# A three-layer graph network: fetching edge lists three nodes at a time, where one block's odd edges are summed, and which engine divides

## The chip, the cores and the metric

The kernel runs on one core of a Trainium2 chip. The core has five engines, each with an instruction queue of its own that it works off in order: TensorE (PE: matmuls, with weight loads shown as PEld), VectorE (DVE), ScalarE (ACT), GpSimd (POOL) and SyncE (SP). SP and ACT issue plain transfers, POOL issues gathers, which fetch one row of a table for each of 128 partitions. The time is in device microseconds for one execution. Before the change it is 3873.78 us, the median of nine runs (3866.43 to 3889.36).

## The reference

The inputs are 6250 nodes with 256 features, 100,000 edges (`src`, `dst`, random and sorted by `dst`), and the weights of three attention layers. Each layer sums, over the edges that end in a node, rows of their source nodes, weighted by a softmax over those edges:

```
xl, xr = x @ Wl, x @ Wr                      # 4 heads of 64 (GATv2, two layers)
e      = leaky_relu(xl[src] + xr[dst])
logits = sum over a head of e * att
alpha  = softmax of logits over the edges with the same dst
out    = sum over those edges of alpha * xl[src], + b
x      = layernorm(x + gatv2(elu(gatv2(x))))   # edges of a node to itself added
x      = layernorm(x + gat(x))                 # 8 heads of 32, softmax again
```

The kernel sums over a node's edges with unnormalised exponentials and divides once by their sum. So "the division" below is 256 numbers per node, multiplied by four reciprocals (one for each head), and not a division of each edge.

## The kernel before

**Blocks and columns.** Nodes are sorted by their number of edges, most first, and cut into 49 blocks of 128. A block lays its nodes on the 128 partitions. Block b has `cols[b]` columns, one edge of every node in each: 27 in block 0, and fewer in the later ones. A node's list can hold CM = 38 sources. Block 0 has some nodes with more than 27 edges; those surplus edges have no column (at most 128 in all, FEW = 11 a node) and are done on the side, one edge to a partition: `find_few` (L1240), `few_logits` and `few_sum` (L1293). Places in a list that no edge fills name an extra row (`far`) made so that its weight comes out as zero.

**The prologue, `make_plan` (L712).** The order of its instructions is written out by hand, and each engine follows it. It computes:
- the number of edges of each node (`count`, [128 x 49]). A node stands at partition `node & 127`, column `node >> 7`; `part` splits a node number in this way, and one-hot matmuls into `ph` add the counts up;
- where each node's edges begin in the sorted `src` (`begin_i`, L993), by a matmul over partitions and a running sum over the 49 columns;
- the lists: 49 gathers on POOL (L998), one for each column, each with 38 numbers for 128 nodes, from `list_d`, a copy of `src` in DRAM;
- each node's place in the order by degree: `key`, one-hots `oh`, running sums `cum`, then `place_f`. ACT's queue writes it as one number to a row of the table `xl1_d` (L1058);
- the reverse, which node stands at which place: one-hots `to_hi` (L1071), `given` (L1076), `to_lo` (L1080) and 49 matmuls into `pp` give `node_i`;
- `lacking` (L1006) marks the list places that no edge fills, `fill` (L1013, L1016) puts `far` there with a predicated copy and writes the lists to `near_d` through SP's queue, nine columns (1152 nodes) at a time, six times. A row of `near_d` is the list of one node (38 numbers) with its 256 features behind it, so that one gather fetches both;
- 49 `tables` (L834 to L846): a block of x is transposed and multiplied by Wl1, and written to `xl1_d`. They are placed in groups between the other work;
- checks that the lists and columns suffice (`wrong`, `bad`, summed over partitions by a matmul into `pb`; `many`, L1114; `fits`, L1116), and the weights of the other products (`right`, `left`).

**The layers, `tile_by_degree`.** POOL fetches a node's list row (`near_r`, L1607), and then column by column the rows of the sources (`g`, L1235): 128 rows of 1 KB to a gather, into tiles of up to nine columns, nine tiles in all. A tile is free for new gathers when all readers of its old content are through. For each block of the first two layers:
- DVE: maximum with `xr` (leaky relu in another form), times `att`, sum over each head (L1508 to L1510): the logits `lg`; then the largest logit of a node, `top` (L1374);
- ACT: exponentials of the four heads (L1381), which also give their sums `den`; DVE takes the reciprocal (L1585);
- DVE multiplies the rows by their weights in place (L1412); ACT does this for the last few columns of the block (L1411, four multiplications a column);
- PE adds the columns up, one matmul with the identity for each (L1419), into `acc`, for which there is one buffer.

The block before is finished inside the next one. ACT computes `h = acc * den` with four multiplications, one for each head (`scaled`, L1539), from PSUM; DVE adds the bias (L1546) or, in the second layer, x (L1660). In `layer2` this is called through `middle()`: after the logits, and ahead of `weights`, so on ACT's queue it stands ahead of the exponentials. In block 1 `middle()` also does `few_sum` for block 0 ahead of it: ACT copies the surplus edges' weights, a matmul brings them to one edge a partition (`few_w`, L1298), three DVE operations (L1303 to L1307) weight the rows, and a matmul (L1311) adds the result to `acc`. The third layer has the same structure, with 8 heads, and its sums and its division on DVE.

Of the kernel before, what the change touches and what calls it, by code (L numbers as in the profile page):

```python
# [714 lines left out]
def make_plan(  # L715
# [21 lines left out]

    one = ctx.enter_context(tc.tile_pool(name="plan_one", bufs=1))
# [7 lines left out]
    list_d = dram.tile([-(-E // CM) * CM + CM], I32, name="list_d")  # L746
# [124 lines left out]
    if rest:  # L871
# [9 lines left out]
    nothing = filled_tile("nothing", [1, list_d.shape[0] - E], 0, I32)  # L881
# [3 lines left out]
    nc.scalar.dma_start(list_d[E:].unsqueeze(0), nothing)  # L885
    nc.scalar.dma_start(
        list_d[:E].rearrange("(a b) -> a b", a=a), src.rearrange("(a b) -> a b", a=a)
# [4 lines left out]
    ranks = iota("ranks", [P, CM], [[1, CM]])  # L892
    ones = filled_tile("ones_f", [P, P], 1.0)
# [48 lines left out]
    for what in "lar":  # L942
# [4 lines left out]
    nc.vector.tensor_scalar(  # L947
        part[:, 0, :], run_i, SHIFT, P - 1, op0=OP.logical_shift_right, op1=OP.bitwise_and
    )
    nc.vector.tensor_single_scalar(part[:, 1, :], run_i, SHIFT + 7, op=OP.logical_shift_right)  # L950
# [27 lines left out]

    pc = ps.tile([P, 2, NB], F32, name="pc", tag="ph")
    nc.tensor.matmul(pc[:, 0, :], ones, count, start=True, stop=True)  # L980
    nc.tensor.matmul(pc[:, 1, :], above, count, start=True, stop=True)
# [3 lines left out]
    block = one.tile([P, NB], F32, name="block")  # L985
    nc.vector.tensor_copy(block, pc[:, 0, :])
    upto = one.tile([P, NB], F32, name="upto")
    nc.vector.tensor_tensor_scan(upto, ones_k[:, :NB], block, 0.0, op0=OP.mult, op1=OP.add)
    from_f = one.tile([P, NB], F32, name="from_f")
    nc.vector.tensor_sub(from_f, upto, block)  # L990
    nc.vector.tensor_add(from_f, from_f, pc[:, 1, :])
    begin_i = one.tile([P, NB], I32, name="begin_i")
    nc.vector.tensor_scalar(begin_i, from_f, float(E), 0.0, op0=OP.min, op1=OP.max)  # L993
    near = one.tile([P, NB, CM], I32, name="near")
    no = one.tile([P, NB, CM], I32, name="no")
    listed = list_d.rearrange("(a b) -> a b", b=CM)
    for k in range(NB):
        nc.gpsimd.indirect_dma_start(  # L998
            out=near[:, k, :], out_offset=None, in_=listed,
            in_offset=bass.IndirectOffsetOnAxis(ap=begin_i[:, k : k + 1], axis=1),  # L1000
        )
    spans = [(k, min(NB, k + 9)) for k in range(0, NB, 9)]

    def lacking(k0, k1):
        shape = [P, k1 - k0, CM]
        nc.vector.tensor_tensor(  # L1006
            no[:, k0:k1, :], ranks[:, None, :].to_broadcast(shape),
            count[:, k0:k1].unsqueeze(2).to_broadcast(shape), op=OP.is_ge,
        )

    def fill(k0, k1):
        shape = [P, k1 - k0, CM]
        nc.vector.copy_predicated(  # L1013
            near[:, k0:k1, :], no[:, k0:k1, :], far[:, None, :].to_broadcast(shape)
        )
        nc.sync.dma_start(  # L1016
            near_d[k0 * P : k1 * P, :CM].rearrange("(k p) c -> p k c", p=P).bitcast(I32),
            near[:, k0:k1, :],
        )


    tables(1)
# [3 lines left out]
    )  # L1026
    ohf = oh.rearrange("p k b -> p (k b)")
# [3 lines left out]
    for c0, c1 in cuts:  # L1031
        pk = ps.tile([P, 512], F32, name="pk", bufs=2)
        nc.tensor.matmul(pk[:, : c1 - c0], ones_b, ohf[:, c0:c1], start=True, stop=True)
        nc.vector.tensor_tensor_scan(
            cum[:, c0:c1], ones_k[:, : c1 - c0], pk[:, : c1 - c0],
            cum[:, c0 - 1 : c0] if c0 else 0.0, op0=OP.mult, op1=OP.add,
        )
    tables(2)
    for c0, c1 in cuts:
        pk = ps.tile([P, 512], F32, name="pk", bufs=2)  # L1040
        nc.tensor.matmul(pk[:, : c1 - c0], less, ohf[:, c0:c1], start=True, stop=True)
        nc.vector.tensor_add(cum[:, c0:c1], cum[:, c0:c1], pk[:, : c1 - c0])
    tables(12)
# [13 lines left out]
    with nc.allow_non_contiguous_dma(reason="one number to a row"):  # L1057
        nc.scalar.dma_start(  # L1058
            xl1_d[:NP, W2:].rearrange("(b p) w -> p b w", p=P), place_f.unsqueeze(2)
        )  # L1060
# [6 lines left out]
    nc.sync.dma_start(xl1_d[NP:], nobody[:, 0, : W2 + 1])  # L1067

# [15 lines left out]
    for b in range(NB):  # L1084
        nc.tensor.matmul(pp, to_lo[:, b, :], given[:, b], start=b == 0, stop=b == NB - 1)
    for k in spans:
        lacking(*k)
    fill(*spans[0])
    fill(*spans[1])
# [3 lines left out]
        node_i, got[:, 1, :], float(P), got[:, 0, :], op0=OP.mult, op1=OP.add  # L1093
# [4 lines left out]
    wrong = one.tile([P, KE + NB + 1], F32, name="wrong")  # L1098
    nc.vector.tensor_tensor(wrong[:, : KE - 1], dst_e[:, : KE - 1], dst_e[:, 1:], op=OP.is_gt)
    nc.vector.tensor_tensor(wrong[:, KE - 1 : KE], dst_e[:, KE - 1 :], next_e, op=OP.is_gt)  # L1100
    nc.vector.tensor_tensor(wrong[:, KE : KE + NB], got[:, 2, :], most, op=OP.is_gt)
    nc.vector.tensor_scalar(
        wrong[:, KE + NB :], upto[:, NB - 1 :], float(E), None, op0=OP.not_equal
# [6 lines left out]
    tables(4)  # L1110
    pb = ps.tile([P, 2], F32, name="pb", tag="ph")
    nc.tensor.matmul(pb, ones, bad, start=True, stop=True)
    many = one.tile([P, 1], F32, name="many")
# [3 lines left out]
    right(0)  # L1117
    left(1, nc.vector)
    right(1)
    fill(*spans[2])  # L1120
# [6 lines left out]
    fill(*spans[3])  # L1127
# [10 lines left out]
    for k in spans[4:]:  # L1138
        fill(*k)
# [3 lines left out]
def tile_by_degree(  # L1143
# [149 lines left out]
    def few_sum(work, ps, acc, wt, S, H, width, first):  # L1293
# [511 lines left out]
```

## Time and profile before

| what | value |
|---|---|
| median of 9 runs | 3873.78 us (3866.43 to 3889.36) |
| the profiled execution | 3868.99 us, its span 3867.1 us |
| mean granted TensorE clock | 0.67 |
| prologue: first list gather, last list gather's end, first instruction of the layers on POOL | 40.25, 114.1, 154.82 us |
| layer 1, blocks 0 to 48 | about 205 to 1530 us |
| layer 2 | about 1530 to 2730 us |
| layer 3 | to 3867 us |
| division on ACT (L1539) | 392 instructions, 92.4 us |
| exponentials (L1381) | 392 instructions, 117.5 us |
| DVE before the reciprocals (L1585) | 77.1 us idle over 98 blocks |
| transfers over the span | 395.63 MB, 102 GB/s |

The layers' times are those at which DVE computes `top` of their first block. In a row of the groups, the numbers after the count are the busy time in us, the mean time of one instruction in ns, and the time that the engine stood idle just before them with what ended most of it. In a row of the timeline they are the start, the duration (of all x-many together), engine, line and operation, and in brackets the idle time before with what ended it. "issue" means that nothing is seen that the engine waited for, "remote" that the releaser is not known.

### The profile page before, as it was taken

Reading aid. Unit: us, or ns where it says so; the run is one execution under the profiler, and the core shown is the slowest. Engines: PE = TensorE matmul, PEld = TensorE weight load, DVE = VectorE, ACT = ScalarE, POOL = GpSimd, SP = SyncE. Lnnn points to the kernel's source line nnn. Section 1 sums busy time; section 2 is a strip of 40 time slices with the busy share of each in tenths; the row PEclk is TensorE's granted clock in tenths of the full one; section 3 lists DMA queues with packets and bytes.
Section 4 is the critical chain, followed back from the end, with each engine's and each line's share of the span. In section 5 each row is a group of like instructions: output and inputs, shape, how many; then the busy total and the mean of one; then the engine's idle time right before and its main releaser. Section 6 shows DMA issues by size and latency. Waiting matters only on the chain.

```text
span 3867.1 us, 23945 instructions
## 1 busy us (share of the span) xinstructions
PE 1514.0 (39%) x5129; PEld 1123.4 (29%) x5130; DVE 2801.1 (72%) x2550; ACT 1187.1 (31%) x4568; POOL 2535.4 (66%) x2613
## 2 busy tenths in 40 slices
PE   5325565556676663455644556554000000000000
PEld 4214444434554542344433444443000000000000
DVE  6248897758888876798877889985776565656665
ACT  2114444434455542344434444553000000000000
POOL 6466666666666654666666666653777777777774
PEclk8657788778888886677766767776555555555555
DMA  8433333333343333334434444432333333333332
GB/s 189 103 92 101 101 102 99 105 98 102 103 106 102 103 88 95 104 105 109 107 105 109 111 112 109 118 102 69 104 108 101 97 96 96 98 97 96 97 96 58
DMA packets 196126, 395.63 MB, mean 102 GB/s; under 512 B 63036, under 2 KB 115514, under 8 KB 195956
## 3 DMA queue, kind: packets, MB, share of 16 engines
q0 software_dynamic: 122048, 338.04, 33.3%
q1 hardware_dynamic: 66226, 54.22, 4.8%
q10 hardware_dynamic: 7698, 1.74, 0.4%
q8 instruction: 45, 0.74, 0.1%
q14 instruction: 109, 0.89, 0.1%
HBM read 353.82 MB, written 40.42 MB: 102 GB/s over the span
## 4 chain that ended last, share of the span: by engine, by line
issue 26%; POOL 19%; PE 18%; DVE 16%; ACT 10%; another core or an unknown queue 9%; DMA 2%; DVEq 0%; SPq 0%; ACTq 0%; POOLq 0%
POOL g L1235 18%; PE acc L1419 13%; DVE z L1508 4%; DVE z L1509 4%; ACT g L1411 3%; PE pm L1362 3%; DVE lg L1510 3%; ACT wt L1381 2%; DVE g L1412 2%; POOL out L1745 1%; ACT h L1539 1%; DMA g<-xl_d,near_r 1%; DVE weighted L1432 1%; PE pt L1355 1%
## 5 line engine op out<-in xcount | busy, mean ns | idle before, releaser
L1235 POOL DMA_INDIRECT g<-xl_d,near_r x1569 | 1491.1, 950 | 826.2 <-issue 441.9
L1419 PE MATMUL acc<-g,ident 128*128 128x256 f32 x3408 | 1068.1, 477 | 828.2 <-issue 313.2
L1419 PEld LDWEIGHTS acc<-g,ident 128*128 128x128 f32 x3408 | 794.6, 242 | 1095.3 <-issue 519.3
L1235 POOL DMA_INDIRECT g<-whs_d,near_r x766 | 794.2, 1037 | 286.7 <-issue 250.8
L1411 ACT ACTIVATE g<-g,by 128x64 f32<-128x64 f32 x2056 | 561.2, 338 | 459.9 <-issue 456.8
L1508 DVE TENSOR_TENSOR z<-g,pr 128x1820 f32<-128x1820 f32 (+4 forms) x234 | 497.2, 2125 | 31.8 <-remote 10.2
L1509 DVE TENSOR_TENSOR z<-z,at 128x1820 f32<-128x1820 f32 (+4 forms) x234 | 497.5, 2126 | 8.1
L1510 DVE TENSOR_REDUCE lg<-z 128x28 f32<-128x1820 f32 (+4 forms) x234 | 497.3, 2125 | 8.1
L1441 DVE TENSOR_REDUCE acc_v<-weighted 128x256 f32<-128x4096 f32 (+15 forms) x49 | 343.7, 7014 | 16.2 <-remote 8.3
L1412 DVE TENSOR_TENSOR g<-g,wt 128x1792 f32<-128x1792 f32 (+8 forms) x234 | 348.5, 1506 | 5.9 <-ACT sd L1455 2.2
L1391 ACT ACTIVATE wt<-lg 128x128 f32<-128x128 f32 (+17 forms) x49 | 14.0, 285 | 850.8 <-DVE top L1374 347.5
L1715 DVE TENSOR_TENSOR lg<-g,s_r 128x56 f32<-128x56 f32 (+4 forms) x111 | 22.4, 214 | 314.8 <-DMA g<-whs_d,near_r 295.3
L1432 DVE TENSOR_TENSOR weighted<-g,wt 128x1792 f32<-128x1792 f32 (+4 forms) x111 | 226.6, 2056 | 0.1
L1357 ACT COPY xT<-pt 128x256 f32<-128x256 f32 x147 | 54.9, 374 | 504.6 <-PE pt L1355 301.0
L1381 ACT ACTIVATE wt<-lg,top 128x19 f32<-128x19 f32 (+14 forms) x392 | 117.5, 300 | 155.2 <-issue 79.9
L1362 PE MATMUL pm<-wcat,xT 128*128 128x260 f32 x392 | 119.6, 456 | 34.4 <-ACT xT L1357 27.4
L1660 DVE TENSOR_TENSOR h<-h,near_r 128x256 f32<-128x256 f32 x49 | 20.8, 425 | 146.7 <-ACT h L1539 106.1
L1546 DVE TENSOR_TENSOR h<-h,fixed_r 128x256 f32<-128x256 f32 x49 | 20.9, 427 | 142.9 <-issue 62.0
L1362 PE MATMUL pm<-wh_cat,xT 128*128 128x272 f32 x196 | 84.1, 569 | 86.3 <-ACT xT L1357 45.8
L1362 PEld LDWEIGHTS pm<-wcat,xT 128*128 128x128 f32 x392 | 84.4, 227 | 63.0 <-ACT xT L1357 40.7
L1539 ACT ACTIVATE h<-acc,den 128x64 f32<-128x64 f32 x392 | 92.4, 332 | 22.8 <-PE acc L1311 22.8
L1362 PE MATMUL pl<-wcat,xT 128*128 128x260 f32 x196 | 60.9, 437 | 70.8 <-ACT xT L1357 49.2
(232 smaller groups left out, 1563.2 us busy)
## 6 DMA issues: line engine op xcount, KB each, us to landing
g<-xl_d,near_r POOLq DMA_INDIRECT x1569
g<-whs_d,near_r POOLq DMA_INDIRECT x766
whs_d<-row SPq DMA_DIRECT2D x49, 132.0 KB
xl_d<-xl SPq DMA_DIRECT2D x49, 130.0 KB
xl_d<-row SPq DMA_DIRECT2D x49, 130.0 KB
xr_d<-row SPq DMA_DIRECT2D x49, 130.0 KB
two<-xl_d SPq DMA_DIRECT2D x49, 130.0 KB
two<-xr_d SPq DMA_DIRECT2D x49, 130.0 KB
```

Of the source, the lines that this page charges most:

```text
L1235: nc.gpsimd.indirect_dma_start(out=g[:, j + own - s0, :width], out_offset=None, in_=table, in_offset=source(of, b, j),)
L1362: nc.tensor.matmul(pm, xT[:, c, :], w[:, c, :], start=c == 0, stop=c == 1)
L1381: nc.scalar.activation(wt[:, :, h], lg[:, :S, h], AF.Exp, bias=top[:, h : h + 1], accum_out=den[:, h : h + 1],)
L1411: nc.scalar.mul(g4[:, t, h, :], g4[:, t, h, :], by[:, t - m, h : h + 1])
L1412: nc.vector.tensor_mul(g4[:, :m], g4[:, :m], wt[:, s0 : s0 + m, :].unsqueeze(3).to_broadcast([P, m, H, F // H]),)
L1419: nc.tensor.matmul(acc, ident, g4[:, t], start=s0 + t == 0, stop=s0 + t == S - 1 and not more)
L1432: nc.vector.tensor_mul(prod[:, s0 - base : s1 - base, :].rearrange("p t (h d) -> p t h d", h=H), g[:, :n, :F].rearrange("p t (h d) -> p t ...
L1441: nc.vector.reduce_sum(part, prod[:, : s1 - base, :].rearrange("p s f -> p f s"), axis=AX.X)
L1508: nc.vector.tensor_max(z, g[:, :n, :W2], xr[:, None, :].to_broadcast([P, n, W2]))
L1509: nc.vector.tensor_mul(z, z, at[:, None, :].to_broadcast([P, n, W2]))
L1510: nc.vector.reduce_sum(lg[:, s0:s1, :], z.rearrange("p t (h d) -> p t h d", h=H2), axis=AX.X)
L1539: nc.scalar.mul(per_head(h, H2)[:, k, :], per_head(acc, H2)[:, k, :], den[:, k : k + 1])
```

## The change

*The lists.* A node now stands at partition `node // 49`, column `node % 49`; the quotient is had by a multiplication and a shift (`by`, `down`). So the 49 nodes of a partition are consecutive, and their edges lie one after another in `list_d`. Where a partition's edges begin is a matmul over the row sums (`total`), where a node's begin within the partition a running sum (`within`). POOL fetches 17 pieces for each partition, each for three nodes (SEGS, STEP) and of 133 numbers (LONG). A node's list starts somewhere in the piece: at the mean of 16 edges a node before it, and an offset of −32 to 31 from that. DVE moves each list to its place: `off_i` is the offset in 6 bits; copies with the mean's shift, and for each bit from 32 down to 1 a predicated copy that shifts those lists by that power of two whose bit is set (`moved`). 32 zeros stand ahead of the edges in `list_d` for this. A check is added that no offset is out of range. `fill` writes to `near_d` from POOL's queue instead of SP's, nine consecutive nodes to a partition, and all six fills stand together after the shifts. The tables are spread anew: 12 of them behind the write of `place_f` instead of ahead of it, and all that remain ahead of the check's matmul `pb`. The loads for the third layer's weights and the biases come behind all tables.

*The columnless edges.* `few_sum` runs in block 0, behind its weights, and its closing matmul into `acc` behind the block's sums. In the third layer the same function is called, and the matmul follows it as before.

*The division.* `end` multiplies `acc` by `den` with one DVE instruction for all four heads, behind `weights` of the next block; `middle` and `scaled` are gone.

```diff
-    list_d = dram.tile([-(-E // CM) * CM + CM], I32, name="list_d")
+    list_d = dram.tile([-(-(LEAD + E) // LONG) * LONG + LONG], I32, name="list_d")
...
-    nc.vector.tensor_scalar(
-        part[:, 0, :], run_i, SHIFT, P - 1, op0=OP.logical_shift_right, op1=OP.bitwise_and
+    nc.vector.tensor_single_scalar(part[:, 1, :], run_i, SHIFT, op=OP.logical_shift_right)
+    nc.vector.tensor_single_scalar(part[:, 0, :], part[:, 1, :], float(by), op=OP.mult)
+    nc.vector.tensor_single_scalar(part[:, 0, :], part[:, 0, :], down, op=OP.logical_shift_right)
+    nc.vector.scalar_tensor_tensor(
+        part[:, 1, :], part[:, 0, :], -float(NB), part[:, 1, :], op0=OP.mult, op1=OP.add
     )
-    nc.vector.tensor_single_scalar(part[:, 1, :], run_i, SHIFT + 7, op=OP.logical_shift_right)
...
-    for k in range(NB):
-        nc.gpsimd.indirect_dma_start(
-            out=near[:, k, :], out_offset=None, in_=listed,
+    piece_of = one.tile([P, SEGS, LONG], I32, name="piece_of")
+    listed = list_d.rearrange("(a b) -> a b", b=LONG)
+    for k in range(SEGS):
+        nc.gpsimd.indirect_dma_start(
+            out=piece_of[:, k, :], out_offset=None, in_=listed,
             in_offset=bass.IndirectOffsetOnAxis(ap=begin_i[:, k : k + 1], axis=1),
...
+    for k in range(STEP):
+        for first_at in (0, LEAD):
+            data = piece_of[:, :, MEAN * k + first_at : MEAN * k + first_at + WIDE]
+            if first_at == 0:
+                nc.vector.tensor_copy(moved[:, :, k, :], data)
+            else:
+                nc.vector.copy_predicated(
+                    moved[:, :, k, :],
+                    bit[:, BITS - 1, :, k : k + 1].to_broadcast([P, SEGS, WIDE]), data,
+                )
...
+    for k in range(BITS - 2, -1, -1):
+        n = CM + (1 << k) - 1
+        nc.vector.copy_predicated(
+            every[:, :, :n], bits[:, k, :].unsqueeze(2).to_broadcast([P, SEGS * STEP, n]),
+            every[:, :, 1 << k : (1 << k) + n],
+        )
...
-        nc.sync.dma_start(
-            near_d[k0 * P : k1 * P, :CM].rearrange("(k p) c -> p k c", p=P).bitcast(I32),
+        nc.gpsimd.dma_start(
+            near_d.rearrange("(p k) c -> p k c", k=NB)[:, k0:k1, :CM].bitcast(I32),
             near[:, k0:k1, :],
...
     for k in spans:
         lacking(*k)
-    fill(*spans[0])
-    fill(*spans[1])
+        fill(*k)
+    tables(4)
...
-    tables(4)
+    tables(NB)
     pb = ps.tile([P, 2], F32, name="pb", tag="ph")
...
-                middle()
...
-            def scaled(acc, den):
+            def end(b, acc, den):
                 h = work.tile([P, F], F32, name="h")
-                for k in range(H2):
-                    nc.scalar.mul(
-                        per_head(h, H2)[:, k, :], per_head(acc, H2)[:, k, :], den[:, k : k + 1]
-                    )
-                return h
+                nc.vector.tensor_mul(
+                    per_head(h, H2), per_head(acc, H2),
+                    den.unsqueeze(2).to_broadcast([P, H2, D2]),
+                )
...
-                rows, cut, wt, new = attend(b, middle)
+                rows, cut, wt, new = attend(b)
                 if b:
-                    rest = end(b - 1, h[0])
+                    rest = end(b - 1, acc, den)
                 else:
-                    few_wt = wt[0]
+                    few = few_sum(work, pst, wt[0], cols[0] + 1, H2, D2 + 1)
...
                 acc = weighted_sum(
                     ps1, rows, cut, wt, H2, D2 + 1, between, b == 0,
                 )
+                if b == 0:
+                    nc.tensor.matmul(acc, edges_of, few, start=False, stop=True)
```

## The prediction

> **What bounds the kernel now.** I read the totals and the groups by line first, then three stretches of the timeline: the prologue, block 1 of the first layer, and an ordinary block.
>
> ```profile
> PE 1514.0 (39%) x5129; PEld 1123.4 (29%) x5130; DVE 2801.1 (72%) x2550; ACT 1187.1 (31%) x4568; POOL 2535.4 (66%) x2613
> ...
> L1235 POOL DMA_INDIRECT g<-xl_d,near_r x1569 | 1491.1, 950 | 826.2 <-issue 441.9
> ...
> L1539 ACT ACTIVATE h<-acc,den 128x64 f32<-128x64 f32 x392 | 92.4, 332 | 22.8 <-PE acc L1311 22.8
> ```
>
> No engine is full: DVE is busiest with 72%. One gather of 128 rows takes POOL 0.95 us and the next starts 0.30 us later, 1.25 us in all. POOL's row shows 442 us of "issue", about that gap, and most of the rest is waiting for row tiles to come free. The last row is the division that the change moves: 98 blocks of four multiplications on ACT, 92.4 us.
>
> The prologue, from the timeline:
>
> ```profile
> 63.83 6.68 DVE L1080 TENSOR_TENSOR to_lo<-each_lo,to 128x6272 bf16<-128x6272 bf16 x1
> ...
> 65.04 6.29 POOL L998 DMA_INDIRECT near<-list_d,begin_i  x1 [0.30 <-issue]
> ...
> 113.17 0.95 POOL L998 DMA_INDIRECT near<-list_d,begin_i  x1 [0.30 <-issue]
> 116.89 0.16 DVE L1114 TENSOR_SCALAR many<-pb 128x1 f32<-128x1 f32 x1 [33.47 <-remote]
> ...
> 154.82 0.24 POOL L1182 IOTA numbers<- 128x128 f32 x1 [40.70 <-DMA near_d<-near]
> ```
>
> The 49 list gathers end at 114.1. DVE has waited 33.47 us for a check, the tables that lie ahead of that check crawl meanwhile, and SP queues the last list writes behind table writes until 147. The layers start only when these have landed, at 154.82. Which engine stands still while the gathers run shows in the busy times by stretch (columns: stretch, its length, busy time and instructions of PE, PEld, DVE, ACT and POOL, granted clock, DMA share, GB/s):
>
> ```profile
> 80.00:117.00 37.00, 6.08 (x19) 4.04 (x17) 3.28 (x10) 2.48 (x7) 25.89 (x28) 0.57 0.39 85
> 117.00:155.00 38.00, 20.96 (x98) 17.18 (x98) 3.80 (x20) 13.90 (x52) 0.18 (x1) 0.77 0.73 145
> ```
>
> With the gathers over, PE does three times as much in the same time.
>
> Block 1 of the first layer, then an ordinary block:
>
> ```profile
> 282.12 0.37 ACT L1357 COPY xT<-pt 128x256 f32<-128x256 f32 x1 [48.41 <-remote]
> ...
> 286.57 0.20 DVE L1303 TENSOR_TENSOR few_weight<-few_w,few_hot 128x44 f32<-128x44 f32 x1 [49.32 <-issue]
> ...
> 288.29 0.93 ACT L1539 ACTIVATE h<-acc,den 128x64 f32<-128x64 f32 x4 [5.69 <-PE acc L1311]
> ```
> ```profile
> 1066.07 0.94 ACT L1539 ACTIVATE h<-acc,den 128x64 f32<-128x64 f32 x4
> ...
> 1067.05 0.42 DVE L1546 TENSOR_TENSOR h<-h,fixed_r 128x256 f32<-128x256 f32 x1 [3.51 <-issue]
> ...
> 1081.89 0.95 POOL L1235 DMA_INDIRECT g<-xl_d,near_r  x1 [3.57 <-ACT g L1411]
> ```
>
> In block 1 the chain xT, few_w, few_part, acc, h holds the exponentials until 289.09. In the ordinary block the exponentials wait for the division, and DVE for both; but POOL, before its next tile, waits 3.57 us for ACT's row multiplications.
>
> **The change, part by part.** The sum starts from the profiled execution, 3868.99 us (span 3867.1, 1.9 around it). It lies 4.8 us (0.12%) below the median of 3873.78; 0.3%, about what can be told from no change, is 11.6 us.
>
> *List gathers.* 49 gathers of 38 numbers become 17 of 133, and 32 x 1.25 = 40 us of POOL time go. begin_i comes from slightly other small operations, still near 39.8. The longer rows move 1.16 MB against 0.95 MB; the price per gather stays at 0.95 us, since it is the same for list rows and 1 KB rows. Five gathers stay held by the large bf16 operations (6.29 us beside to_lo), so the 17th comes near 72.6 and lands near 75, instead of 114.
>
> *Shifts on DVE (new).* Three copies and three predicated copies of 1173 elements, then five predicated copies of 2703 to 1938, 11,016 together. The fills give the price: 342 elements in 0.54 (at 72.78, L1013), the later 1178 elements in four operations in 1.60, so about 1.04 ns an element and 0.2 us each. That is 6 x 1.2 + 12.5 = 20 us, from 75 to 95; the nine operations on 51 numbers (2 us) lie before. Six lackings and fills (0.41 + 0.5 each) end at 101–102.
>
> *List writes, from SP to POOL.* Six writes, the first near 97, each of up to 1152 runs of 152 bytes; POOL has nothing else to do. No plain POOL transfer is in the trace. Bounds: one gather's 0.95 us per write, 5.7 us in all; or 0.95 us per 128 runs, 49 x 0.95 = 46.6 us. These end at 103 and 144; I take 35 us, nearer the second, as a gather of 128 rows is the only thing of this kind seen. With a few us to land, the layers start at about 134, against 154.82. The Trainium skill, DMA: Bandwidth & Descriptors, section "Anatomy of one DMA", says that many descriptors can be emitted before their generation costs noticeably; by that rule the 5.7 us would hold and the sum would be 29 us lower, and no run here shows it yet. The Trainium skill, SBUF — State Buffer, in its warning on VectorE blocking DMA, would have kept these writes off POOL: descriptors cannot be written while certain VectorE operations run; here the row at 65.04, stretched to 6.29 us beside a bf16 product, agrees that POOL can be held, though that page does not count such a product among the blocking operations.
>
> *Tables, checks.* 21 of the 49 tables remain at 76. They run at 1.09 us each once undisturbed (after 117), so they end at 99–115 and are covered by the writes; without that cover they would set the start at about 120. The number writes (6272 of four bytes) go out near 53 instead of 64.26, into a stretch whose DMA share is already 0.96; this may slow tables by some us. The two added check operations cost 0.3 us and hide under the tables. SP loads the weights later, covered until the third layer. The transfers before 155, 24.28 MB at the 218 GB/s of the first 50 us, need 111 us, so no start before that. Prologue: 154.8 − 134 = −20; at the two ends of the write price −41 (start 114) and −8 (tables crawling, start 147).
>
> *Columnless edges.* Moved into block 0. Its copy, matmuls and three DVE operations (0.85 us) run at about 207, ahead of a wait of 49.32 us, and disappear in it. In block 1, xT at 282.12 is followed by the exponentials at about 282.5 instead of 289.09: −7. In the second layer the same step had no such wait: 0 to −1, taken 0. Layer 3 only changes where the matmul is written: 0.
>
> *Division.* DVE gains 98 operations of 128x256 at the 0.43 us of the rows L1546 and L1660, 42 us. They lie after `top`, while ACT runs the exponentials (1.85 us for four heads), with 0.85 of other DVE work: 1.28 < 1.85. Where DVE is the later, its reciprocal waits 0.8 to 1.2 us for them now (77.1 us over 98 blocks), so this cover is measured; without it the 42 us would be paid in full. Behind the division on DVE queue the adds, reciprocal and weighting; it waits for acc, but ACT's division waited 22.8 us over all blocks, all of it in block 1, so acc is not late. ACT loses 0.94 us per block ahead of the exponentials. In the 65 or so blocks where DVE waits 1 to 5 us for h, the weighting starts up to 0.94 sooner: −61 at most. But there POOL gives the period: blocks of 16 gathers take 23.4–23.6 us, 16 x 1.25 + 3.6, and of 14 gathers 20–21. ACT's row multiplications (L1411) follow each other at 1.4 us beside gathers and at 0.26 when POOL stands (1080.92 to 1082.2: five in 1.30). Starting 0.94 sooner gets 0.7 of them more done before POOL stops, worth 0.2 us a block: −13. I take −25, nearer the POOL end.
>
> Sum: 3868.99 − 20 − 7 − 25 = **3817**.
>
> **Rivals.**
> 1. *Cheap writes, ACT on the path.* POOL's part costs 6 us and every ACT-late block gains 0.94. For: DVE's waits before L1660 name ACT's h for 106 us. Against: the period fits 1.25 per gather. 3868.99 − 41 − 7 − 61 = 3760.
> 2. *No earlier start.* The table stall returns beside POOL's writes and the layers start at about 155. For: all crawls lie beside POOL transfers. Against: six writes, not 49 gathers. 3868.99 − 7 − 25 = 3837.
> 3. *The cover is only partial.* 33 blocks where DVE is the later pay 0.43 each (+14), the others gain nothing, prologue −8: 3868.99 − 8 − 7 + 14 = 3868, no change. Against: the reciprocal's measured wait.
> 4. *Slower: the writes cost POOL more than the gathers saved.* If 128 runs cost what a gather beside DVE work cost here (2.26 at 59.90), 49 x 2.3 = 113 us, POOL ends at 210 and the start is 55 us later: 3868.99 + 55 − 32 = 3892. It eats all gains from 1.83 us per 128 runs, a start at 187, and shows as slower from 2.06. For: POOL prices go by rows. Against: DVE is nearly idle by then.
>
> **Chances.** Forecast 0.45; rival 1 0.14; rival 2 0.13; rival 3 0.12; rival 4 0.16. Forecast and rivals 1 and 2 are faster: 0.72. Same 0.12, slower 0.16. The forecast's own range is 3795 to 3840. The wide range leaves out the far part of rival 1 and most of rival 4: 3770 to 3882.
>
> **What would show it.** 17 list gathers ending by 75; predicated copies between 75 and 96; six POOL transfers whose duration settles the largest unknown, and `numbers` at 134. The few sums in block 0, and exponentials of block 1 right behind xT. In ordinary blocks the DVE division inside the exponentials, a reciprocal wait shrunk to about 0.4, and POOL's 3.6 us wait only slightly shorter. I am wrong if `numbers` starts after 154.8, if DVE waits for acc at its division, or if blocks of 16 gathers take more than 23.5 us.

## The result, and the profile after

The changed kernel takes 3826.89 us (median of 10 runs, 3819.76 to 3843.11), the kernel before 3874.01 us (31 runs): a ratio of 0.9881, with a 95% interval of 0.9866 to 0.9895, so 47 us less. The profiled execution took 3824.77 us with a span of 3822.9 us, against 3868.99 and 3867.1 before: 44.2 us less of each. The forecast, 3817, was 52 below its profiled execution. The bracketed figures behind later times are the ratio to the kernel before and its 95% interval.

First the totals and the groups of the changed kernel (line, engine, operation, tiles, count; busy us and mean ns; idle us before and what ended most of it). L1300, L1476 and L1446 are the gathers, ACT's row multiplications and the exponentials, formerly L1235, L1411 and L1381.

```profile
PE 1484.2 (39%) x5129; PEld 1106.8 (29%) x5130; DVE 2859.7 (75%) x2674; ACT 1101.9 (29%) x4176; POOL 2510.1 (66%) x2588
...
L1300 POOL DMA_INDIRECT g<-xl_d,near_r x1569 | 1489.9, 950 | 827.9 <-issue 456.1
...
L1476 ACT ACTIVATE g<-g,by 128x64 f32<-128x64 f32 x2056 | 558.1, 337 | 427.9 <-issue 424.6
...
L1602 DVE TENSOR_TENSOR h<-acc,den 128x256 f32<-128x256 f32 x98 | 40.8, 416 | 184.4 <-remote 162.0
L1638 DVE RECIPROCAL den<-den 128x4 f32<-128x4 f32 x98 | 17.4, 178 | 215.0 <-ACT wt L1446 123.4
```

ACT lost 85 us of busy time and DVE gained 59, yet POOL's waiting between its gathers is the same 828 us (826 before). The division costs DVE 0.42 us each, as priced.

The prologue, from the timeline (start, duration, engine, line, operation, idle time before):

```profile
71.81 0.95 POOL L1016 DMA_INDIRECT piece_of<-list_d,begin_i  x1 [0.30 <-issue]
...
77.93 0.81 DVE L1113 COPY moved<-piece_of 128x1173 int32<-128x1173 int32 x1 [8.21 <-DMA piece_of<-list_d,begin_i]
78.77 1.54 DVE L1115 COPY_PREDICATED moved<-bit,piece_of 128x1173 int32<-128x1173 int32 x1
...
84.86 14.10 DVE L1123 COPY_PREDICATED moved<-bit,moved 128x2703 int32<-128x2703 int32 x5
...
100.25 5.84 POOL L1143 DMA_DIRECT2D near_d<-moved  x6 [27.50 <-DVE moved L1140]
...
122.17 0.24 POOL L1247 IOTA numbers<- 128x128 f32 x1 [16.08 <-DMA near_d<-moved]
```

The 17th gather ends at 72.8. The shifts run from 77.9 to 99, and POOL hands out all six list writes in 5.84 us. They need another 16 us to land, and the layers start at 122.17 instead of 154.82. The busy times by stretch (stretch, length, then PE, PEld, DVE, ACT, POOL with their instructions, granted clock, DMA share, GB/s) show that PE and ACT go on working now between 80 and 117:

```profile
80.00:117.00 37.00, 19.14 (x89) 15.26 (x88) 29.37 (x48) 12.97 (x50) 5.84 (x6) 0.82 1.05 202
117.00:155.00 38.00, 9.30 (x27) 6.55 (x27) 16.04 (x22) 1.67 (x5) 24.85 (x29) 0.59 0.53 103
```

PE did 6.08 us of work in that first stretch before and does 19.14 now; the DMA engines are full (1.05) where they were at 0.39.

Block 1 of the first layer, and an ordinary block:

```profile
236.88 0.37 PE L1420 MATMUL pt<-ident,near_r 128*128 128x128 f32 x1 [1.73 <-issue]
...
249.96 0.42 DVE L1602 TENSOR_TENSOR h<-acc,den 128x256 f32<-128x256 f32 x1 [37.41 <-remote]
250.00 0.37 ACT L1422 COPY xT<-pt 128x256 f32<-128x256 f32 x1 [47.85 <-remote]
250.27 0.32 ACT L1446 ACTIVATE wt<-lg,top 128x26 f32<-128x26 f32 x1
```
```profile
1006.23 0.41 DVE L1602 TENSOR_TENSOR h<-acc,den 128x256 f32<-128x256 f32 x1
...
1009.47 0.38 ACT L1422 COPY xT<-pt 128x256 f32<-128x256 f32 x1
1009.74 0.31 ACT L1446 ACTIVATE wt<-lg,top 128x16 f32<-128x16 f32 x1
...
1011.54 0.18 DVE L1638 RECIPROCAL den<-den 128x4 f32<-128x4 f32 x1 [4.09 <-ACT wt L1446]
...
1027.67 0.95 POOL L1300 DMA_INDIRECT g<-xl_d,near_r  x1 [3.71 <-ACT g L1476]
```

In block 1 the long wait for xT is there as before (47.85 us), but the exponentials follow it at once. By the profile PE had ended the transpose at 237.25, and ACT's copy of it began 12.8 us later. DVE waited here too, 37.41 us at its division.

In the ordinary block DVE has divided by 1006.6, and then waits 4.09 us for the exponentials: before, DVE waited for h, now it waits at the reciprocal. The exponentials do come sooner behind ACT's copy of xT, 0.27 us after its start, where it was 1.06 before:

```profile
1065.81 0.38 ACT L1357 COPY xT<-pt 128x256 f32<-128x256 f32 x1
...
1066.87 0.33 ACT L1381 ACTIVATE wt<-lg,top 128x16 f32<-128x16 f32 x1
```

But POOL's wait for its next tile is 3.71 us against 3.57, and POOL's blocks of 16 gathers in the first layer take 23.5 to 23.7 us, where they took 23.4 to 23.9.

Set side by side by the start of `top`, the saving grows like this: 32.6 us at block 0 of the first layer (204.7 to 172.1), 38.6 at block 2 (318.9 to 280.3), 45.0 at the first block of the second layer (1531.5 to 1486.5), 45.7 at the first of the third (2733.4 to 2687.7), 44.2 at the end. So the prologue gave 32.6, the columnless edges 6.0, and everything after them, where only the division differs, about 6. These are one profile of each kernel, and executions of the changed kernel lie between 3819.76 and 3843.11, so the last 6 cannot be told from this scatter.

### The profile page after: what moved, and what is told of

Read it like the earlier page. It is cut to its first block, busy times and chain, and to the rows that moved or that the text cites. A ratio compares the mean times of both kernels' runs of the same rounds, so it can differ in the third digit from the quotient of the medians.

```text
span 3822.9 us, 23565 instructions
## 1 busy us (share of the span) xinstructions
PE 1484.2 (39%) x5129; PEld 1106.8 (29%) x5130; DVE 2859.7 (75%) x2674; ACT 1101.9 (29%) x4176; POOL 2510.1 (66%) x2588
## 5 line engine op out<-in xcount | busy, mean ns | idle before, releaser
L1300 POOL DMA_INDIRECT g<-xl_d,near_r x1569 | 1489.9, 950 | 827.9 <-issue 456.1
L1484 PE MATMUL acc<-g,ident 128*128 128x256 f32 x3408 | 1024.4, 462 | 797.9 <-remote 300.6
L1484 PEld LDWEIGHTS acc<-g,ident 128*128 128x128 f32 x3408 | 769.4, 233 | 1045.4 <-issue 464.6
L1300 POOL DMA_INDIRECT g<-whs_d,near_r x766 | 795.5, 1039 | 282.6 <-issue 248.4
L1476 ACT ACTIVATE g<-g,by 128x64 f32<-128x64 f32 x2056 | 558.1, 337 | 427.9 <-issue 424.6
L1602 DVE TENSOR_TENSOR h<-acc,den 128x256 f32<-128x256 f32 x98 | 40.8, 416 | 184.4 <-remote 162.0
L1638 DVE RECIPROCAL den<-den 128x4 f32<-128x4 f32 x98 | 17.4, 178 | 215.0 <-ACT wt L1446 123.4
L1446 ACT ACTIVATE wt<-lg,top 128x19 f32<-128x19 f32 (+14 forms) x392 | 116.1, 296 | 167.1 <-issue 98.7
L1427 PE MATMUL pm<-wcat,xT 128*128 128x260 f32 x392 | 136.4, 506 | 70.9 <-ACT xT L1422 65.3
L1427 PEld LDWEIGHTS pm<-wcat,xT 128*128 128x128 f32 x392 | 94.6, 254 | 106.3 <-ACT xT L1422 81.3
L1427 PEld LDWEIGHTS pm<-wh_cat,xT 128*128 128x128 f32 x196 | 46.1, 260 | 147.2 <-ACT xT L1422 93.8
L1800 POOL DMA_INDIRECT out<-y,node_i x49 | 50.5, 1031 | 49.7 <-ACT y L1528 36.0
```

Of the source, the lines that this page charges most:

```text
L1300: nc.gpsimd.indirect_dma_start(out=g[:, j + own - s0, :width], out_offset=None, in_=table, in_offset=source(of, b, j),)
L1427: nc.tensor.matmul(pm, xT[:, c, :], w[:, c, :], start=c == 0, stop=c == 1)
L1446: nc.scalar.activation(wt[:, :, h], lg[:, :S, h], AF.Exp, bias=top[:, h : h + 1], accum_out=den[:, h : h + 1],)
L1476: nc.scalar.mul(g4[:, t, h, :], g4[:, t, h, :], by[:, t - m, h : h + 1])
L1484: nc.tensor.matmul(acc, ident, g4[:, t], start=s0 + t == 0, stop=s0 + t == S - 1 and not more)
L1800: put = nc.gpsimd.indirect_dma_start(out=out[:, :], out_offset=node(b), in_=y, in_offset=None, bounds_check=N - 1, oob_is_err=False,)
```

## The experiments

They ran on three chips, and each is compared only with the kernel before on its own chip. Those differ: the kernel before takes 3357.82 us on the first (27 runs), 3855.42 on the second (17) and 3852.80 on the third (22). The first chip turned out to be a test of its own. There ACT's row multiplications follow each other at 0.24 us without exception; on the other two, and in the profile before, many of them stand apart (worked out from their starts: 537 of 1960 intervals are 0.6 us or more before, none on the first chip). The same in the groups, kernel with only the division moved, first chip and third:

```profile
L1235 POOL DMA_INDIRECT g<-xl_d,near_r x1569 | 1487.9, 948 | 515.6 <-issue 424.3
...
L1411 ACT ACTIVATE g<-g,by 128x64 f32<-128x64 f32 x2056 | 500.0, 334 | 0.0
```
```profile
L1235 POOL DMA_INDIRECT g<-xl_d,near_r x1569 | 1491.6, 951 | 810.3 <-issue 443.4
...
L1411 ACT ACTIVATE g<-g,by 128x64 f32<-128x64 f32 x2056 | 548.2, 337 | 340.4 <-issue 336.2
```

These instructions take as long on both; the idle time before them differs, 0 against 340 us on ACT and 516 against 810 on POOL. I call a chip of the second kind *slowed*.

**Each part alone (first chip, not slowed).** The kernel before with the new prologue; with `few_sum` in block 0; with the division in `end`:

```diff
 # lists only: make_plan of the changed kernel, tile_by_degree of the one before
 # columnless edges only
+                    few = few_sum(work, pst, wt[0], cols[0] + 1, H2, D2 + 1)
...
+                if b == 0:
+                    nc.tensor.matmul(acc, edges_of, few, start=False, stop=True)
 # division only
-                    if b:
-                        h.append(scaled(acc, den))
...
-                    rest = end(b - 1, h[0])
+                    rest = end(b - 1, acc, den)
```

> The prologue of the change alone, the layers as before. In the changed kernel the first instruction of the layers on POOL came at 122.2 us instead of 154.8. If the prologue carries most of the gain and nothing is given back, this kernel is 30 to 35 us below the one before, and the first instruction of the layers stays at 122. Rival: part of an earlier start is lost again in block 0 and 1, where before DVE and ACT waited nearly 50 us for something that an earlier start does not bring forward: then the gain is 15 to 25.

> The columnless edges moved to block 0 alone. The forecast's term says 7 us less, all of it in block 1 of the first layer. Rival: the wait of block 1 for xT does not end sooner and its length follows the POOL burst, so that what stands behind xT is hidden: 0 to 2 us less.

> The division on DVE alone; the columnless edges stay in block 1. If ACT's 0.94 us ahead of the exponentials lie on the path in the 65 late blocks, 25 to 60 us less. If POOL's gathers and the wait for ACT's row multiplications set the period there, 5 to 13 us less. Rival on the other side: DVE pays 0.42 us in blocks where it is the later, 0 to 14 us more.

Measured: lists 3353.77 (0.9988, 0.9979 to 0.9997), columnless edges 3356.43 (0.9996, 0.9987 to 1.0005), division 3350.97 (0.9979, 0.9970 to 0.9988): 4, 1 and 7 us less. So the lists, worth most on the first measurement, are worth almost nothing here, and neither of my two explanations foresaw it. The stretch 80 to 117 tells why; it is the old prologue, on the first chip and on the third:

```profile
80.00:117.00 37.00, 23.21 (x108) 18.26 (x108) 5.10 (x20) 13.80 (x52) 26.14 (x28) 0.80 0.85 198
```
```profile
80.00:117.00 37.00, 7.77 (x24) 4.81 (x21) 7.13 (x27) 4.87 (x24) 26.05 (x28) 0.56 0.50 98
```

Where nothing is slowed, the old prologue has no stall: its 28 gathers run in this stretch just the same, the tables are made beside them, and the layers start at 125.65. The new prologue starts them at 120.65. On the slowed chip the old one starts them at 155.34.

The division's 7 us are not spread over the blocks there either. Against the kernel with only the columnless edges moved, `top` of block 48 comes at 1221.9 (1221.6), of the next layer's first block at 1271.2 (1273.9), of the third layer's first at 2326.9 (2334.0). Two ends of layers are shorter by 3 and 3.4 us (49.3 against 52.3, 43.1 against 46.5), and within the layers DVE sets the period, and the division fits into its wait: it takes 40.6 us over the 98 blocks, and the idle time before the reciprocals falls from 89.8 to 51.6 us.

**Half of ACT's share (first chip).** The columns that ACT weights go from a third of a block to a sixth:

```diff
-                few = min(S // 3, cut[-1][1] - cut[-1][0] - 1) if b + 1 < NB else 0
+                few = min(S // 6, cut[-1][1] - cut[-1][0] - 1) if b + 1 < NB else 0
```

> The changed kernel with half as many columns weighted by ACT (a sixth of a block's columns instead of a third), so ACT has about 1000 row multiplications fewer and DVE about 2.5 columns more a block. If the period is a burst of gathers and then a wait for ACT's row multiplications, POOL's wait shrinks and blocks where DVE has slack get shorter by 1 to 2 us: 30 to 90 us less. If DVE is the bound or nearly so, it pays 2.5 columns x 0.29 us x 98 blocks = 70 us, and the kernel is up to 70 us slower.

3420.76 us (1.0188, 1.0173 to 1.0204), 63 us above the kernel before, and about 75 above what the three parts alone add up to (3357.82 − 12; the changed kernel itself was not run on this chip). DVE's work is added in full: without the slowing DVE is the bound.

**The changed kernel, and its layers alone (second chip, slowed).** The second kernel has the changed `tile_by_degree` and the prologue as before.

> The changed kernel again, beside the kernel before on the same chip. The kernel before took 3874 us in the first measurement and 3358 us in the first experiments; where it takes 3358, ACT's row multiplications follow each other at 0.24 us throughout, where it takes 3874 a quarter of them stand 0.7 to 2.1 us apart. If that slowing beside POOL's gathers is what the new lists avoid, then the changed kernel is 44 to 50 us below on a chip that shows it, and only about 12 us below (4 for the lists, 1 for the columnless edges, 7 for the division) on one that does not. Rival: the three gains were not additive, and together they give 20 us or more on either.

> The changed layers (columnless edges in block 0, division on DVE) with the prologue as before. On a chip with the slowing: 10 to 15 us less than before, since the start of the layers stays at 154.8 us, and the rest of the 47 us belongs to the lists. On a chip without it: 6 to 9 us less, the sum of the two parts alone.

3815.72 (0.9910, 0.9892 to 0.9929) and 3846.03 (0.9979, 0.9963 to 0.9995): 39.7 and 9.4 us less, each a little under what was expected. So the lists give 30 us on this chip against 4 on the first. The layers start at 125.26 against 152.75, again the size of the gain. For the columnless edges the two profiles agree with the first measurement: from `top` of block 0 to that of block 2 pass 107.8 and 107.6 us, against 114.2 before, and 114.2 in the kernel with only the division moved (third chip).

**The queue of the list writes (second chip).**

```diff
-        nc.gpsimd.dma_start(
+        nc.sync.dma_start(
             near_d.rearrange("(p k) c -> p k c", k=NB)[:, k0:k1, :CM].bitcast(I32),
```

> The changed kernel with the list writes on SP's queue instead of POOL's. In the changed kernel POOL took 5.84 us for all six writes, and they landed 16 us later, with the DMA engines fully busy from 80 to 117. If the queue does not matter and the transfers do, the start of the layers stays within 3 us of 121. If SP's queue, where the writes stand among those of the tables, makes them wait as in the kernel before, the start is 5 to 15 us later.

```profile
101.16 10.16 SPq L1143 DMA_DIRECT2D near_d<-moved  x6
...
128.93 0.24 POOL L1247 IOTA numbers<- 128x128 f32 x1 [55.14 <-DMA near_d<-xt]
```

3824.19 us (0.9915, 0.9898 to 0.9933), and the start at 128.93: 3.7 us later, just outside the 3 us that I had allowed. The 10.16 us of SP's queue are not all its own price: the first four writes take 0.36 to 0.37 us each and stand about 1 us apart, as DVE's fills end, and only the last two take longer (1.82 and 4.29), where POOL takes about 1 us for each. But SP works off its queue in order, so the stores of the tables behind the writes wait as well: ACT stands 24.48 us for them (99.1 to 123.56), which it does not in the changed kernel. The time is 8.5 us higher, but the intervals of the two overlap. So the queue matters by less than 4 us of start.

**Longer shifts (second chip).**

```diff
+    for _ in range(3):
     for k in range(STEP):
         for first_at in (0, LEAD):
```

> The changed kernel with the first three copies and three predicated copies of the shifts done three times, 14 us more on DVE (2 x 7.0) ahead of the list writes. If DVE's shifts set the start of the layers, it comes 14 us later (about 135). If the transfers of the tables set it, which fill the DMA engines until 117, it comes 0 to 6 us later.

```profile
114.56 5.84 POOL L1144 DMA_DIRECT2D near_d<-moved  x6 [41.06 <-DVE moved L1141]
...
134.05 0.24 POOL L1248 IOTA numbers<- 128x128 f32 x1 [13.65 <-DMA near_d<-moved]
```

The writes begin 13.3 us later than in the changed kernel (114.56 against 101.25), the layers 8.8 us later (134.05 against 125.26), and the time is 6.5 us higher (3822.24; 0.9925, 0.9909 to 0.9942), with intervals that overlap. The start lies between the two expectations: two thirds of a longer shift are paid, and a third is taken back, since the writes, issued later, land sooner after their issue.

**Do the gathers make the stall? (third chip, slowed.)** To the kernel with the writes on SP, 32 gathers of 38 numbers are added behind the 17, into a tile that nobody reads:

```diff
+    spare = one.tile([P, NB - SEGS, CM], I32, name="spare")
+    short = list_d[: list_d.shape[0] // CM * CM].rearrange("(a b) -> a b", b=CM)
+    for k in range(NB - SEGS):
+        nc.gpsimd.indirect_dma_start(
+            out=spare[:, k, :], out_offset=None, in_=short,
+            in_offset=bass.IndirectOffsetOnAxis(ap=begin_i[:, k % SEGS : k % SEGS + 1], axis=1),
+        )
```

> The changed kernel with the list writes on SP and 32 further gathers of 38 numbers on POOL behind its 17, into a tile that nobody reads; POOL holds nothing up then, and the layers wait for nothing of them. On a chip with the slowing, if the gathers themselves slow the tables, the stall of the kernel before comes back: PE's busy time between 80 and 117 us falls from 17 to under 10 us, and the layers start at 140 to 155 instead of 129; the time is 12 to 25 us above that of the kernel with the writes on SP. Rival: the stall came from SP's queue or the check's wait and not from the gathers; then the start stays at 129. On a chip without the slowing the start stays in either case.

```profile
80.00:117.00 37.00, 22.66 (x112) 18.52 (x112) 29.83 (x44) 11.71 (x36) 29.04 (x19) 0.82 1.02 125
```
```profile
74.47 0.38 PE L848 MATMUL pt<-ident,xt 128*128 128x128 f32 x2
...
79.60 0.37 ACT L850 COPY xT<-pt 128x256 f32<-128x256 f32 x1 [9.68 <-remote]
...
86.42 3.10 POOL L1023 DMA_INDIRECT spare<-list_d,begin_i  x1 [0.30 <-issue]
...
124.75 0.38 ACT L859 COPY xl<-pm 128x260 f32<-128x260 f32 x1 [23.57 <-DMA xl_d<-xl]
...
133.84 0.24 POOL L1254 IOTA numbers<- 128x128 f32 x1 [6.20 <-DMA wh_cat<-in_L_gnn_W]
```

Over the whole stretch the stall did not come back: PE worked 22.66 us in it, the layers started at 133.84, and the time is 3832.28 (0.9946, 0.9928 to 0.9965). The kernel with the writes on SP, on the second chip, started them at 128.93 and has 0.9915; by the ratios the added gathers cost 12 us, with intervals that overlap.

But the added gathers have to be read in three parts. From 73.3 to 79.6 they run undisturbed, at 0.94 to 1.01 us each, and there the tables stand. PE had ended its transposes by 74.85, and ACT copied the first of them at 79.60. The same stretch in this kernel, and in the kernel with more share for ACT, which ran on the same chip without added gathers:

```profile
73.30:79.60 6.30, 1.55 (x12) 1.15 (x9) 1.08 (x2) 0.00 (x1) 4.78 (x5) 1.00 1.09 341
```
```profile
73.30:79.60 6.30, 5.15 (x29) 4.22 (x28) 0.65 (x1) 2.88 (x9) 0.06 (x1) 1.00 1.08 350
```

From 79.65 until about 100 the gathers are held beside DVE's shifts, 1.9 to 3.1 us each, and the tables run: PE works 20.58 of the 21 us from 79.6 to 100.6. After that the gathers run at 0.94 again, but ACT waits 23.57 us for table stores. The kernel with the writes on SP has this wait without any added gather (24.48), so the third part says nothing about the gathers. In the one part that can tell, the tables stood while the gathers ran undisturbed and went on when they were held. That speaks for my theory, and neither the list writes on SP (from 100.6) nor the check lies in that part. It is 6.3 us of one profile, and it holds for a slowed chip alone: on the first chip the tables run beside undisturbed gathers.

**The division alone, and ACT's share up and down (third chip).** The division alone and half the share are the kernels from above; more share is `S // 2` in the changed kernel.

> The division on DVE alone once more, for a chip with the slowing (without it, it was 7 us less, most of that where the layers change). Both parts of the layers together were 9 us less there, so 3 to 9 us less is left for the division, far from the 25 of the forecast; rival: the columnless edges cost something there and the division gives 15 or more.

> The changed kernel with half of a block's columns weighted by ACT instead of a third (as far as the last tile reaches). Without the slowing, DVE is the bound (idle 1 us a block) and ACT is idle 8 us a block; half the share cost 1.9%, so 2 to 3 columns more on ACT save 0.29 us each on DVE: 40 to 80 us less than the changed kernel. With the slowing, ACT's instructions stand 0.7 to 2.1 us apart while POOL gathers, and the wait before POOL's next tile grows: 20 to 100 us more.

> Half the ACT share once more, for a chip with the slowing (without it, it was 63 us slower than the kernel before). If there the number of ACT's instructions sets how long POOL waits, the blocks get shorter although DVE works 70 us more: 0 to 60 us less than the changed kernel. If DVE's work is added to the period all the same, 30 to 70 us more.

The division alone: 3851.36 (0.9989, 0.9974 to 1.0003), 1.4 us less, below what was expected and not to be told from nothing. More share for ACT: 3821.75 (0.9924, 0.9907 to 0.9940), the same as the changed kernel within the intervals (0.9910, on the second chip), though ACT does 504 row multiplications more; 20 to 100 us more was expected, and that was wrong. Half the share: 3844.06 (0.9972, 0.9957 to 0.9988), about 24 us above the changed kernel by the ratios, where the first chip paid 75. The groups of the last one:

```profile
L1300 POOL DMA_INDIRECT g<-xl_d,near_r x1569 | 1492.0, 951 | 829.3 <-issue 535.4
...
L1476 ACT ACTIVATE g<-g,by 128x64 f32<-128x64 f32 x960 | 245.7, 334 | 58.8 <-issue 58.8
```

ACT's idle time before its row multiplications is down to 59 us, and POOL still waits 829 us between its gathers; the trace names PE's `acc` for 111.7 us of it, where it named ACT's row multiplications for 115.0 in the changed kernel. What is named changes from profile to profile: for the same changed kernel on the second chip it is PE's `acc` with 85.8 ahead of them. So the multiplications were named in the waits, but their number alone does not set the period. The test is not a clean one, since the columns that ACT gives up are about 73 us of work more for DVE (2932.3 us busy against 2859.7).

None of the variants is below the changed kernel, each taken by its ratio to the kernel before on its own chip.

## Why the prediction was right, and where its terms were not

The direction and the size were right: 3817 forecast, 3826.89 measured, inside the likeliest case's own range. The sum was 52 and the profiles differ by 44.2, but two of its three terms were off, one of them about 13 us too small and the other about 19 too large. That the sum came so near is luck: the errors cancelled.

*Prologue, 20 forecast, 32.6 measured.* The times of the 17 gathers (the last at 72.6, measured 71.81), the fills at 101 to 102 (104.5) and the shifts (six operations of about 1.2 us each, measured 0.8 and 1.54; 12.5 us for the five stages, measured 14.10) were near. The price of 1.04 ns an element did not fit the second row that it was taken from, where 1178 elements took 1.60 us; the five stages took 1.28 ns an element. Mis-sized was the price of the list writes. I took 35 us, near the rows' bound of 46.6, because a gather of 128 rows was the nearest thing in the trace; POOL took 5.84, the other bound (5.7). The sentence of the Trainium skill, DMA: Bandwidth & Descriptors, section "Anatomy of one DMA", that many descriptors can be emitted before their generation costs noticeably, holds here: six writes of 1152 runs (the last of 512) took about 0.97 us each, as long as a gather of 128 rows. The forecast gives two starts for this rule, 105 (134 less 29) and 114 (its cheap end), and both were too early: writes that are handed out still have to get through DMA engines that stayed full (share 1.01 to 1.17 from 106 to 122), which took 16 us, and the fills ended 2.5 later. The forecast's bound of 111 from 218 GB/s was no bound either, since 265 GB/s went through between 80 and 100. Rival 4, that POOL's writes eat the gain, is excluded; the queue matters by 3.7 us of start, in favour of POOL. Rival 1 had the writes right, and its 61 us for the division wrong.

*What the lists really removed.* I priced the prologue as POOL's time: 40 us of gathers against shifts and writes. The first chip shows that this is not where the gain comes from, for there the same 40 us of gathers go and only 4 us of time come of it. What goes is the stall between 80 and 117, in which PE works 6 to 8 us on a slowed chip and 21 to 23 on the first. My reading that the tables crawl in that stretch and would not in the new order was right, and rival 2 (it returns beside POOL's writes) is excluded by the 19.14 us of PE there. What does not hold is my reading that DVE's check waits for the tables ahead of it. PE had done the check's matmul, and the tables before it, by 88.8, and DVE went on at 116.89 (the row of `many`):

```profile
88.37 0.42 PE L1112 MATMUL pb<-bad,ones_f 128*128 128x2 f32 x2
```

That is 28.1 us between the end of the matmul and DVE; in the kernels with the old prologue it is 9.1 and 18.5 us on the other slowed chips and 0.04 on the first. So at this wait the result arrives late; it is not work ahead of it that holds it up. That undisturbed gathers on POOL bring it about on a slowed chip is supported by the one stretch in which added gathers ran alone; why such a chip does this stays open.

*Columnless edges, 7 forecast, 6.0 measured*, by block starts, and 6.0 to 6.7 in the seven further profiles of slowed chips that have the step. The mechanism is right on a slowed chip: xT is late, and what stood behind it is gone. On the first chip xT is not late, and the step is worth 1.4 us with an interval that holds zero.

*Division, 25 forecast, 1 to 7 measured.* That its 42 us on DVE are covered was right on the chip where DVE is the bound: it pays 40.6 us there, and the reciprocals wait 38.2 less. Rival 3 is excluded by it. Wrong was the step that ACT's 0.94 us ahead of the exponentials are worth something in the late blocks. I had bounded it by 13 (POOL gives the period) and 61 (ACT on the path) and took 25; alone it gave 1.4 (interval 10 less to 1 more), and DVE's waits moved without becoming shorter. Before they were 416.0 us (49.3 at the columnless edges, 289.6 for h, 77.1 at the reciprocals); in the changed kernel they are 404.3 (184.4 at the division, 4.9 behind it, 215.0 at the reciprocals).

One of the forecast's own signs of being wrong came true in this: DVE does wait for `acc` at its division, over 1 us in 15 blocks, and the reciprocals wait 2.2 us on the mean, not 0.4. The forecast had read from ACT's 22.8 us at its division that `acc` is not late. But in ACT's queue the copies of xT stand ahead of the division, and they had waited 504.6 us already; a wait at the head of a queue hides the waits behind it. So even the lower bound, which let ACT's sooner start shorten POOL's wait by 0.2 us a block, was at the upper edge of what was found. Half and more of ACT's share speak against that bound's mechanism: ACT's row multiplications end the wait by the profile, but taking them away or adding to them leaves POOL's waiting at 810 to 829 us. What sets it on a slowed chip is not shown. What the division does give comes at the ends of layers, 3 us each on the first chip, where no later block covers them.

## What to carry to other kernels

A busy POOL queue was priced here as time of its own; the larger part of the gain came from engines that stood still beside it, so read in the stretch which engines stop and start again, and take the price from that stretch. An engine that the waits name (here ACT's row multiplications before POOL's next tile) need not be what sets the period: change its work by half before building a term on it. And an engine that hardly waits at an instruction may have done its waiting just ahead of it: look at what the instruction needs, not only at the wait on its row. When a price has two bounds far apart and the nearest row is another kind of operation, the operation's own kind decides; a gather's cost per row did not carry over to a plain write.

## What was not expected of the hardware

The same kernel takes 3358 us on one chip and 3853 to 3874 on others, 15% more. Row multiplications (334 and 337 ns) and the gathers of the first two layers (948 and 951 ns) are equally long. What differs most is the time between instructions of ACT and PE. On the slowed chips ACT's row multiplications come in a quick run of 0.24 us each and then stand 0.7, 1.4 or 2.1 us apart, the profile giving no cause but "issue". PE's results reach ACT late: ACT's copy of xT began up to 22.5 us after PE's transpose had ended, over 2 us in 16 of the 116 copies that ACT waited for in the kernel before, and at most 0.1 us on the first chip (with the new prologue 3.0, once). In the third layer the gathers themselves are longer, 1040 against 950 ns, which is 69 us over 766 of them.

None of the runs shows what makes a chip slowed. Of the 537 long intervals 401 overlap a gather of POOL, and the others end at most 5.4 us behind one; but most of the quick ones overlap gathers too (1158 of 1423), so a gather alone does not make an interval long. In the prologue added gathers brought the stall back only for as long as they ran undisturbed. The consequence for judging a change is large: the lists are worth 30 us on one kind of chip and 4 on the other.

POOL's gathers are held by more than one kind of DVE work. Beside the bf16 comparison `to_lo` (6.68 us) a gather took 6.30 us in the changed kernel, and beside the plain and predicated copies of 32-bit integers the added gathers took 1.9 to 3.1 us instead of 0.94 (2.2 to 3.1 beside predicated copies alone). The Trainium skill, SBUF — State Buffer, in its warning on VectorE blocking DMA, names VectorE operations in a two-port mode, an fp32 copy for one, as what locks POOL out of writing descriptors; the second number goes the same way, though the warning does not name predicated copies. The first number is of a comparison of two tensors (the forecast called it a product), which that warning does not name either.
